# The query projection of six pairs of batches as seven block products, on one Trainium2 core

## The chip, the core and the metric

The kernel runs on one core of one Trainium2 chip. The core has five engines with a queue each: TensorE (PE; its weight loads are listed apart as PEld), VectorE (DVE), ScalarE (ACT), GpSimd (POOL) and SyncE (SP, which here only issues transfers). The metric is the device time of one execution in microseconds (us). Of before there are three timed runs and one profiled execution.

## The reference

All tensors are fp32. For each of 16 batches, with 100 rows `hidden` of 640 and 722 rows of 384, the last 4 of which are the tokens `ca` and the other 718 `enc`:

```python
query = hidden_states @ Wq                 # 100 x 640, 8 heads of 80
keyt, valt = enc @ Wk, enc @ Wv            # 718 x 640
hs = _mha(query, keyt, valt)
ca_q1 = jnp.einsum('btc,th->bch', ca, Wq_ca)[:, indices, :]     # 100 x 640
ca_hs1 = _mha(ca_q1, hidden_states, hidden_states)
ca_hs2 = _mha(ca_hs1 @ Wq, ca @ Wk_ca, ca @ Wv_ca)
out = (hs + ca_hs2) @ Wout + b_out + hidden_states
```

`_mha` is softmax attention by heads. The change concerns the first line, `hidden_states @ Wq`.

## The kernel before

The kernel is one loop over the 16 batches (`for b in range(B)`, line 1236), written for one order: from there on each engine runs its instructions in the order in which the program names them (`manual_schedule`, line 1235). TensorE, VectorE, ScalarE, Pool and SP meet only in semaphores that the framework sets where a buffer is written, read or given free.

One turn of the loop does, for batch b, the scores (`scores`, three groups of keys), the maximum over them (`Maximum`, `top`), their subtraction and exponential (`subtract`, `exponential`), the values (`Values`, `vv.go`), and for batch b + 1 the keys (`Keys`, `kk.go`, and `last_keys`). Keys and values are already computed by sums of blocks: `enc_sums` (line 481) makes thirteen sums of blocks of the encoder rows on Pool, into slots 7 to 14 of the tile `enc`, slots 0 to 6 of which come from memory by transfers (`load_enc`). That tile has two buffers: the one of batch b + 2 becomes free when the value products of batch b have read it. The output of pairs of row blocks is also made by sums (`Last.sums`, `project_pair`), in the turns after batches 2, 5, 7, 10 and 12 (`PAIRS`).

The second attention, over the 4 tokens, is the class `Second`. Its scores are made on Pool (`scores1`, lines 798 and 805), its first maximum on VectorE (`softmax1`, lines 700 to 730: a transpose, a reduction, two short groups of reductions, a spread copy, a transpose back; and the subtraction of line 815), its values on Pool (`values2`, lines 892 and 899: a product for each token and a sum). `load` issues the transfers of the first two tokens' values from Pool's queue; those of the other two are issued from SP's queue as tokens are used up.

**The queries.** Two batches share them. In each odd batch b the queries of the pair p + 1 (batches b + 1 and b + 2) are made (lines 1435 to 1438), after `last_keys` and, where there is one, `project_pair`, and before the attention product `a_ps` of line 1456. Just ahead of them in the program stand the key masks `keys(m_next)` and `enc_sums(enc_next)`, both on Pool alone. `queries` is called for five groups of 128 output columns. Each is five matmuls, one for each 128 of the 640 contracted rows, with a weight tile of 128 x 128 and both batches' rows, 2 x 100, as moving columns:

```python
for c in range(HC):
    nc.tensor.matmul(q_ps[...], wq_sb[:, c, n * P : (n + 1) * P], xT[:, :, c, :], ...)
```

Columns 0 to 511 hold the first 64 columns of each head, and go by a copy on ScalarE into `qp`; the last 128 hold the other 16 of each head, and go into `qz` by two products with a mask. `xT` holds both batches' rows, transposed, and `wq_sb` the weights.

PSUM is eight banks: two pairs (`pair`), two of `psumk`, two of `psum1`. The queries before take theirs from the last two in turn.

Other matmuls already use halves of the columns: `QC` cuts the attention's 100 rows into 0 to 63 and 64 to 99, and the preparation of the tokens' keys (line 1128) uses 64-column weight tiles at 0 and 64.

Of the kernel before, what the change touches and what calls it, by code (L numbers as in the profile page):

```python
# [18 lines left out]
P = 128  # L19
# [107 lines left out]
def kernel(  # L127
# [60 lines left out]
    def hs2_tile(name):  # L188
        return main.tile([P, H], F32, tag="hs2", name=name)
# [361 lines left out]
                )  # L551


    def chunk_keys(n, banks, weights, enc):
# [197 lines left out]
    class Second:  # L752
# [56 lines left out]
        def softmax1(self, n=8):  # L809

            if not self.top:
                self.top = Maximum(e1, f"1_{self.b}", self.b - 2 in PAIRS)
            self.top.go(n)
            if self.top.over is not None:
                nc.vector.tensor_tensor(e1[:S], e1[:S], self.top.over[:S], ALU.subtract)
# [64 lines left out]
            )  # L880
            self.p2 = p2

        def values2(self, behind=None):

            b, p2 = self.b, self.p2
            self.hs2 = hs2_tile(f"hs2_{b}")[:S]
            sums = self.hs2.rearrange("p (h d) -> p h d", h=NH)
            for t in range(T):
# [347 lines left out]
    for b in range(B):  # L1236
# [5 lines left out]
        def loads():  # L1242

            if b == 0:
                nc.sync.dma_start(
                    out=wout_sb, in_=wout.rearrange("(c p) n -> p c n", p=P)
                )
            if b + 2 >= B:
                return None, None
            x_next = xT_at[0] if b % 2 else load_x(p + 1)  # L1250
            xT_at[0] = x_next
            return Second(b + 2, x_next), load_enc(b + 2)
# [74 lines left out]
        elif b + 1 < B:  # L1327
# [59 lines left out]
            second_next, enc_next = loads()  # L1387
            if b + 2 < B:
                m_next = load_m(b + 2)
            subtract(2)  # L1390
# [6 lines left out]
            if last.b in PAIRS:  # L1397
                second.softmax1(3)
                last.project_pair()
                if last.b == max(PAIRS):  # L1400
# [40 lines left out]

# [37 lines left out]
        if b + 2 < B:  # L1479
            second_next.products()  # L1480
            second_next.copy()
        if 0 < b < B - 2:
            mine.turn()
        last = mine
# [55 lines left out]
```

## Time and profile before

| | before |
|---|---|
| timed runs, us | 924.89, 922.83, 924.90; median 924.89 |
| profiled execution, us | 925.05 |
| its span, us | 923.3 |
| granted TensorE clock | 1.00 |
| busy: TensorE, VectorE, Pool, ScalarE | 99%, 74%, 74%, 47% |

A row of the order of time reads: start in us, duration in us, engine, line, operation, output and inputs with their shapes, and how many were merged; in brackets the idle time before it and what ended it. A row of the chain that ended last reads: start, duration, engine, output, line, count. A row of stretches reads: the stretch, its length, then the busy time of TensorE, weight loads, VectorE, ScalarE and Pool with the instructions of each, the granted clock, the share of the transfer engines and what they moved. A matmul in fp32 leaves two records, one for each of two passes. For TensorE a shape such as 128*64 128x64 is rows and columns of the weights, and then rows and moving columns.

### The profile page before, as it was taken

To read this page: it belongs to the slowest core of one execution; us is meant where nothing else is said; L and a number is where in the kernel's file an instruction comes from. 1 tells how busy PE (TensorE), PEld (TensorE's weight loads), DVE (VectorE), ACT (ScalarE), POOL (GpSimd) and SP (SyncE) were. 2 spreads that over 40 slices of the span, in tenths; PEclk is the share of its full clock that TensorE was granted. 3 is DMA by queue.
4 is the path that set the end of the run, shared out by engine and by line. 5 is a ranking of instruction groups with operands and counts; after the bars stand their busy time and mean duration, and the time that the engine had idled before them with its cause. 6 is when DMAs were issued, how large, how long until landed. Compare 5 with 4: busy or idle time off the path is not lost.

```text
span 923.3 us, 26190 instructions
## 1 busy us (share of the span) xinstructions
PE 916.2 (99%) x11290; PEld 772.4 (84%) x11290; DVE 679.9 (74%) x1085; ACT 434.2 (47%) x836; POOL 682.1 (74%) x647
## 2 busy tenths in 40 slices
PE   9999999999999999999999999999999999999998
PEld 6988889788797979888798787988879888797866
DVE  2459795888739896795967859579883898838883
ACT  2234543737327373552636536264641737427341
POOL 5749999788947878497784968757996588956723
PEclk9999999999999999999999999999999999999999
DMA  8822013050300404032030310205031050310201
GB/s 258 262 94 78 25 43 100 2 156 2 103 31 13 116 3 131 3 92 65 19 115 4 103 54 30 76 2 154 3 90 43 2 155 2 104 45 2 82 20 41
DMA packets 49675, 62.85 MB, mean 68 GB/s; under 512 B 14072, under 2 KB 38200, under 8 KB 49560
## 3 DMA queue, kind: packets, MB, share of 16 engines
q1 hardware_dynamic: 45512, 51.49, 18.4%
q0 software_dynamic: 3024, 8.53, 3.0%
q8 instruction: 89, 1.46, 0.7%
q10 hardware_dynamic: 1024, 1.15, 0.4%
q14 instruction: 26, 0.21, 0.1%
HBM read 55.59 MB, written 5.57 MB: 66 GB/s over the span
## 4 chain that ended last, share of the span: by engine, by line
PE 96%; DVE 3%; DMA 1%; issue 0%; POOL 0%; ACTq 0%; DVEq 0%; POOLq 0%
PE a_ps L1456 12%; PE s_ps L609 12%; PE v_psA L434 10%; PE v_psB L434 8%; PE kT_ps L559 8%; PE k_psA L465 8%; PE q_ps L535 7%; PE k_psB L465 6%; PE o_ps L1050 5%; PE v_psC L434 3%; PE k_psC L465 3%; PE v_ps L375 2%; PE v_psD L434 2%; PE v_psE L434 2%; PE y_ps L773 1%; PE k_psD L465 1%
## 5 line engine op out<-in xcount | busy, mean ns | idle before, releaser
L798 POOL TENSOR_TENSOR e<-ca,g 100x800 f32<-100x800 f32 x64 | 97.9, 1540 | 125.1 <-ACT kT L407 82.1
L500 POOL TENSOR_TENSOR enc<-enc 128x240 f32<-128x240 f32 x135 | 109.5, 820 | 18.2 <-DMA enc<-in_enct 11.1
L1258 DVE TENSOR_TENSOR st<-st,over 120x1600 f32<-120x1600 f32 x48 | 119.1, 2482 | 0.0
L1456 PEld LDWEIGHTS a_ps<-vs,st 120*36 120x36 f32 (+3 forms) x3072 | 109.2, 125 | 4.9 <-issue 4.8
L1456 PE MATMUL a_ps<-vs,st 120*36 120x81 f32 (+3 forms) x3072 | 112.0, 233 | 0.0
L434 PE MATMUL v_psA<-wv_sb,enc 128*120 128x320 f32 x352 | 109.3, 433 | 0.0
L899 POOL TENSOR_TENSOR hs<-hs,hs 100x640 f32<-100x640 f32 x48 | 100.6, 2095 | 3.8
L805 POOL TENSOR_TENSOR e<-e,e 100x800 f32<-100x800 f32 x48 | 93.6, 1950 | 3.8
L892 POOL TENSOR_TENSOR hs<-vb,p 100x640 f32<-100x640 f32 x64 | 88.0, 1386 | 5.9 <-DMA vb<-va_d 3.0
L434 PE MATMUL v_psB<-wv_sb,enc 128*120 128x320 f32 x296 | 91.9, 433 | 0.0
L1266 ACT ACTIVATE st<-st 120x1600 f32<-120x1600 f32 x48 | 73.9, 1539 | 37.0 <-DVE st L1258 36.9
L465 PE MATMUL k_psA<-enc,wk_sb 128*128 128x240 f32 x360 | 89.2, 371 | 0.0
L434 PEld LDWEIGHTS v_psA<-wv_sb,enc 128*120 128x120 f32 x352 | 64.2, 183 | 25.0 <-issue 0.5
L465 PEld LDWEIGHTS k_psA<-enc,wk_sb 128*128 128x128 f32 x360 | 67.2, 190 | 15.0
L1270 DVE TENSOR_TENSOR most<-most,st 120x800 f32<-120x800 f32 x64 | 67.6, 1056 | 15.9 <-ACT st L659 14.8
L609 PE MATMUL s_ps<-qp,kT 64*56 64x100 f32 (+1 forms) x3072 | 73.5, 248 | 0.0
L465 PE MATMUL k_psB<-enc,wk_sb 128*128 128x240 f32 x300 | 73.0, 366 | 0.0
L434 PEld LDWEIGHTS v_psB<-wv_sb,enc 128*120 128x120 f32 x296 | 54.1, 183 | 21.9 <-DVE vs L405 0.4
L609 PEld LDWEIGHTS s_ps<-qp,kT 64*56 64x56 f32 (+1 forms) x3072 | 67.1, 130 | 5.5 <-issue 4.2
L965 ACT COPY hsT<-turned_hs 32x160 f32<-32x160 f32 (+7 forms) x244 | 67.7, 278 | 3.0
L535 PE MATMUL q_ps<-xT,wq_sb 128*128 128x200 f32 x400 | 69.1, 333 | 0.0
L535 PEld LDWEIGHTS q_ps<-xT,wq_sb 128*128 128x128 f32 x400 | 67.8, 190 | 1.0 <-issue 0.5
(168 smaller groups left out, 1766.1 us busy)
## 6 DMA issues: line engine op xcount, KB each, us to landing
vb<-va_d POOLq DMA_DIRECT2D x32, 250.0 KB, 3.8
vb<-va_d SPq DMA_DIRECT2D x32, 250.0 KB
enc<-in_enct SPq DMA_DIRECT2D x30, 240.0 KB
enc<-in_enct SPq DMA_DIRECT2D x15, 360.0 KB
xT<-in_xt SPq DMA_DIRECT2D x8, 500.0 KB
rest<-in_enct SPq DMA_DIRECT2D x31, 120.0 KB
xn<-in_x SPq DMA_DIRECT2D x11, 320.0 KB
out<-xn SPq DMA_DIRECT2D x11, 320.0 KB
```

Source lines behind the costliest of these rows:

```text
L434: nc.tensor.matmul(at[0][j][:KN, : H // 2], a_form(self.enc, f)[:, j * KN : (j + 1) * KN], wv_there.get(f, wv_sb[:, W_AT[f]]), start=first ...
L465: nc.tensor.matmul(at[:, i * KT : (i + 1) * KT], wk_sb[:, W_AT[f], i], a_form(self.enc, f), start=(first and i == 0), stop=last, skip_grou ...
L500: nc.gpsimd.tensor_tensor(out, left, right, op)
L535: nc.tensor.matmul(q_ps[:, : 2 * S].rearrange("p (j s) -> p j s", j=2), wq_sb[:, c, n * P : (n + 1) * P], xT[:, :, c, :], start=(c == 0), ...
L609: nc.tensor.matmul(s_ps[at][k0:k1, cols], w, rhs, start=not begun & {(at, k) for k in range(k0, k1, 32)}, stop=last, skip_group_check=True,)
L798: first = nc.gpsimd.tensor_tensor(to, self.ca[:, t, :].unsqueeze(1).to_broadcast([S, NH, S]), g[:, :, t].unsqueeze(2).to_broadcast([S, NH, ...
L805: nc.gpsimd.tensor_tensor(e, e, to, ALU.add)
L892: first = nc.gpsimd.tensor_tensor(to, self.vb[t][:S].rearrange("p (h d) -> p h d", h=NH), p2[:, :, t].unsqueeze(2).to_broadcast([S, NH, D] ...
L899: nc.gpsimd.tensor_tensor(sums, sums, to, ALU.add)
L1258: return nc.vector.tensor_tensor(st[i], st[i], top.over[:KN].unsqueeze(1).to_broadcast([KN, 2, ROWS]), ALU.subtract,)
L1266: nc.scalar.activation(st[i], st[i], AF.Exp, scale=SCALE)
L1456: nc.tensor.matmul(a_v[lo:hi, h % 4], st[i // 2][: KEYS[i], i % 2, h * S + lo : h * S + hi], block(i, h // 4)[: KEYS[i], h % 4], start=(i ...
```

## The change

In the odd batches 3 to 13 (the queries of the pairs 2 to 7) the product over the first 512 of the 640 contracted rows and the first 512 output columns is made of seven block products for eight, after Strassen and Winograd. The blocks are two halves of the contraction (256 rows, v(0, m) and v(1, m) of batch m), two halves of the output columns (W(c, g)), and the two batches. The sums are

- t1 = v(0,1) - v(0,0), t2 = v(1,1) - t1, t4 = v(1,0) - t2, t3 = v(1,1) - v(0,1), each 128 x 200;
- w2 = W'(1,0) - W(0,0), w3 = W(1,1) - w2, then w2 = W(0,1) - w2, each 128 x 512, where W'(1,0) = W(1,0) + W(1,1) is made once on VectorE at the end of batch 1 and stays in `wq_sb`.

All but that one are made on Pool, into the slots of the next `enc` tile that `enc_sums` fills later. The last 128 contracted rows (`rest`) and the last 128 output columns (bank f) are made as before. All matmuls of these queries have weight tiles of 64 columns, at 0 and 64 in turn. Six banks are used: two pairs (f and e, c and d) and both `psumk` (a and b). Banks a and b are read and then accumulated further, so each product that adds to them comes after a read. VectorE adds five times out of PSUM into `qp`.

The order changes with it. In these batches the transfers of `loads` are named ahead of `second.load`, and `enc_sums` comes after the queries. Where there is no `project_pair` (batches 5, 7, 9, `parted`) the sums stand between the third and the fourth token of `values2` on Pool; `second.load` and `keys(m_next)` come after the queries; and `softmax1` stops after three steps, its rest standing behind the read of bank b. In batches 3, 11 and 13 `keys(m_next)` stays ahead and the sums follow it, and `softmax1` is run to its end before.

```diff
+        def sums(self):
+            v = self.v
+            for out, left, right in (
+                (self.t1, v(0, 1), v(0, 0)),
+                (self.t2, v(1, 1), self.t1),
+                (self.w2, wq_block(1, 0), wq_block(0, 0)),
+                (self.t4, v(1, 0), self.t2),
+                (self.t3, v(1, 1), v(0, 1)),
+                (self.w3, wq_block(1, 1), self.w2),
+            ):
+                nc.gpsimd.tensor_tensor(out, left, right, ALU.subtract)
+
+        def product(self, bank, weights, moving, first):
+            steps = [(c, i) for c in range(weights.shape[1]) for i in range(2)]
+            for n, (c, i) in enumerate(steps):
+                for k in (0, 64):
+                    nc.tensor.matmul(
+                        bank[k : k + 64, i * S : (i + 1) * S],
+                        weights[:, c, i * P + k : i * P + k + 64],
+                        moving[:, c],
+                        start=first and n == 0,
+                        stop=n == len(steps) - 1,
+                        skip_group_check=True,
+                    )
+
+        def rest(self, bank, g, m, first):
+            weights = wq_sb[:, 4:, 2 * g * P : 2 * (g + 1) * P]
+            self.product(bank, weights, self.xT[:, m, 4:], first)
+
+        def make(self, tiles, between):
...
+            for ch in range(HC):
+                for k in (0, 64):
+                    nc.tensor.matmul(
+                        full(f)[k : k + 64],
+                        wq_sb[:, ch, 4 * P + k : 4 * P + k + 64],
+                        self.xT[:, :, ch, :],
...
+            for u in range(2):
+                nc.scalar.mul(
+                    qz[:, 0, :, u * S : (u + 1) * S], full(f), qmask[:, u : u + 1]
+                )
+            self.product(a, w(0, 0), v(0, 0), True)
+            nc.scalar.copy(q(0, 0), full(a))
+            self.rest(c, 0, 0, True)
+            self.product(c, w(0, 1), v(1, 0), False)
+            add(c, 0, 0)
+            self.product(a, self.w2, self.t2, False)
+            nc.gpsimd.tensor_tensor(self.w2, w(0, 1), self.w2, ALU.subtract)
+            self.rest(e, 1, 0, True)
+            self.product(e, w(1, 1), self.t4, False)
+            nc.scalar.copy(q(1, 0), full(e))
+            add(a, 1, 0)
+            self.product(b, self.w3, self.t3, True)
+            add(b, 1, 0)
+            self.rest(d, 0, 1, True)
+            self.product(d, self.w2, v(1, 1), False)
+            nc.scalar.copy(q(0, 1), full(d))
+            self.rest(b, 1, 1, False)
+            nc.scalar.copy(q(1, 1), full(b))
+            between()
+            self.product(a, w(1, 0), self.t1, False)
+            add(a, 0, 1)
+            add(a, 1, 1)
...
-            now.values2()
+            parted = b % 2 and b > 1 and last.b not in PAIRS
+            now.values2(None, range(T - 1 if parted else T))
...
-            second.load()
+            mixed = None
+            if b % 2 and b > 1:
+                second_next, enc_next = loads()
+                mixed = Queries(p + 1, xT_at[0], enc_next[0])
+            if parted:
+                mixed.sums()
+                now.values2(None, range(T - 1, T))
+            else:
+                second.load()
...
-            second.softmax1()
+            second.softmax1(3 if parted else 8)
...
-        if 0 < b < B - 2:
-            keys(m_next)
-            enc_sums(enc_next)
         if b % 2 and b + 1 < B:
             xT, tiles = xT_at[0], queries_tiles(p + 1)
-            for n in range(HC):
-                queries(p + 1, xT, tiles, n)
+            if not mixed:
+                for n in range(HC):
+                    queries(p + 1, xT, tiles, n)
+            elif parted:
+                mixed.make(tiles, second.softmax1)
+                second.load()
+            else:
+                keys(m_next)
+                mixed.sums()
+                mixed.make(tiles, second.softmax1)
+        if 0 < b < B - 2:
+            if not mixed or parted:
+                keys(m_next)
+            enc_sums(enc_next)
...
+        if b == 1:
+            nc.vector.tensor_tensor(
+                wq_block(1, 0), wq_block(1, 0), wq_block(1, 1), ALU.add
+            )
```

More of the change, by code (lines that the diff above doesn't have):

```diff
@@ L551, in queries, with wq_block, __init__, v @@
                 )
+    def wq_block(g, c):
+        return wq_sb[:, 2 * c : 2 * c + 2, 2 * g * P : 2 * (g + 1) * P]
+    class Queries:
+        def __init__(self, p, xT, enc):
+            self.p, self.xT = p, xT
+            room = enc[:, len(A_RAW) :].rearrange("p f k -> p (f k)")
+            part = lambda lo, n: room[:, lo : lo + 2 * n].rearrange(
+                "p (c n) -> p c n", c=2
+            )
+            self.w2, self.t1 = part(0, 2 * P), part(4 * P, S)
+            lo = 3 * KT
+            self.w3 = part(lo, 2 * P)
+            self.t3, self.t2, self.t4 = (
+                part(lo + 4 * P + 2 * i * S, S) for i in range(3)
+            )
+        def v(self, c, m):
+            return self.xT[:, m, 2 * c : 2 * c + 2]
+        def sums(self):
[25 more added lines that the diff above has]
+        def make(self, tiles, between):
+            qp, qz = tiles
+            p, v, w = self.p, self.v, wq_block
+            one = pair(f"q_ps1_{p}")
+            two = pair(f"q_ps2_{p}")
+            a, b = psumk(f"q_psA_{p}"), psumk(f"q_psB_{p}")
+            f, e, c, d = one[:, 0], one[:, 1], two[:, 0], two[:, 1]
+            def q(g, m):
+                return qp[:, g, :, m * S : (m + 1) * S]
+            def full(bank):
+                return bank[:, : 2 * S].rearrange("p (i s) -> p i s", i=2)
+            def add(bank, g, m):
+                nc.vector.tensor_tensor(q(g, m), full(bank), q(g, m), ALU.add)
+            for ch in range(HC):
[4 more added lines that the diff above has]
+                        self.xT[:, :, ch, :],
+                        start=(ch == 0),
+                        stop=(ch == HC - 1),
+                        skip_group_check=True,
+                    )
+            for u in range(2):
+                nc.scalar.mul(
+                    qz[:, 0, :, u * S : (u + 1) * S], full(f), qmask[:, u : u + 1]
+                )
+            self.product(a, w(0, 0), v(0, 0), True)
[20 more added lines that the diff above has]
+            add(a, 1, 1)
@@ L812, in softmax1 @@
                 self.top = Maximum(e1, f"1_{self.b}", self.b - 2 in PAIRS)
+            if self.top.over is not None:
+                return
             self.top.go(n)
```

11 lines of the change are left out of this document (7 added, 4 removed).

## The prediction

> **What bounds the kernel now.** I read the page first (span, busy shares, shares of the chain that ended last), then what TensorE waited for, then the chain in order of time around the block of queries, and last the order of time on each engine there.
>
> ```profile
> span 923.3 us, 26190 instructions
> PE 916.2 (99%) x11290; PEld 772.4 (84%) x11290; DVE 679.9 (74%) x1085; ACT 434.2 (47%) x836; POOL 682.1 (74%) x647
> PE 96%; DVE 3%; DMA 1%; issue 0%; POOL 0%; ACTq 0%; DVEq 0%; POOLq 0%
> PE idle_ps L1116 <- DVE idle L1113: 1.1, 1, 1.1
> PE y_ps L773 <- POOL m L745: 0.7, 1, 0.7
> ...
> PE k_psC L465 <- DVE vs L405: 0.4, 2, 0.2
> 253.94 8.46 PE q_ps L535 x50
> 262.40 6.92 PE a_ps L1456 x191
> ...
> 357.60 8.46 PE q_ps L535 x50
> 366.06 6.92 PE a_ps L1456 x191
> ```
>
> TensorE is busy in 916.2 of 923.3 us and is 96% of the chain; its longest waits are three one-off pieces of about 1 us or less, none at the queries. So a microsecond taken from TensorE's own stream is a microsecond of the span, and so is each new wait put into it. The block of queries is 8.46 us, 50 records (25 matmuls, two records each in fp32): 169.2 ns a record. With 200 moving columns that is 2 x 200 cycles of the 2.4 per ns that the granted clock of 1.00 stands for (166.7 ns) and 2.5 ns. The attention product follows at once, at 262.40 and 366.06. The last two rows are batch 5, the others batch 3.
>
> **What the change does to TensorE.** Six of the eight blocks (the odd batches 3 to 13) are redone. Five of the 25 matmuls (the last 128 output columns) keep 200 moving columns, in two 64-column halves. The other 20 become seven block products of four and four remainders of two matmuls of 100 columns, 36 in all, again in halves: 72 matmuls, 144 records. Full-width work falls from 25 x 200 = 5000 to 1000 + 3600 = 4600 columns, 8%. What is left of that hangs on the cost of a 64-column record with 100 moving columns, a shape that does not run now. Three neighbours do:
>
> ```profile
> L1128 PE MATMUL k_ps<-tokens,wk_sb x60: 222/222/270, 20.3 to 22.0; 128*64 128x64 f32 x60
> 366.06:372.98 6.92, 6.92 (x198) 6.92 (x200) 1.67 (x3) 1.50 (x3) 4.74 (x7) 1.00 0.02 5
> 273.08 2.97 PE L609 MATMUL s_ps<-qp,kT 64*64 64x100 f32 x128
> 275.98 0.95 PE L609 MATMUL s_ps<-qz,kT 32*120 32x200 f32 x16
> ```
>
> The first has the same weights (128 rows, 64 columns, both halves in turn) over 64 moving columns: 1.7 us between the first and last of 60 starts, 29 ns each. The second row is the attention product's window: by the code 8 heads x 6 blocks x 2 halves x 2 = 192 records of 81 columns in 6.92 us, 36.0 ns each. Both are N/2.4 + 2.3 ns, so two halves together advance as fast as one full-width record and only the 2.3 ns is paid twice. At N = 100 that is 44.0 ns. The scores give the dear end: 100 columns in four tiles, 128 records from 273.08 to 275.98, 22.7 ns each; a pair of halves as slow as those four is 45.3 ns a record. I take 44.0, the rows of the same tiling. The 200-column halves are 83.3 + 2.3 = 85.6 ns.
>
> One block: 144 x 44.0 = 6.34, and 20 x 85.6 = 1.71, together 8.05 us for 8.46: 0.41 us saved (0.22 at 45.3 ns). Six blocks: 2.46 us, dear end 1.3. Every block still starts after full-width work and ends before the attention's halves.
>
> The row against this is the weight load. *The Trainium skill ("TensorE: Matmul & The Clock Gate", section "LDWEIGHTS (loading the stationary operand)") has a load take its columns over 1.2 per ns, 53.3 ns for 64; were loads one after another, a record could not be faster than that.* In the first row above a load and a matmul of just this shape go by every 29 ns, and 29 is under 44, so loads do not decide here; it stays as a small rival.
>
> **The new waits.** Within a block, counted from its first record and with no wait: the 200-column part ends at 1.71, product one at 2.42, remainder and product on bank c at 2.77 and 3.47, the product with w2 at 4.18, remainder and product on e at 4.53 and 5.23, the one with w3 at 5.94, remainder d 6.29, the product with the second w2 6.99, remainder b 7.34, the last product 8.05. Sums are due at 3.47 (t2, w2), 4.53 (t4), 5.23 (t3, w3) and 6.29 (second w2, which can start only once the product with the first is over, at 4.18). They all come from Pool, in order with its other work:
>
> ```profile
> 249.74 1.54 POOL L1071 TENSOR_TENSOR wout<-wout,wout_sb 128x640 f32<-128x640 f32 x1
> 251.24 1.41 POOL L745 TENSOR_TENSOR m<-mb,hmask 128x64 f32<-128x64 f32 x5
> 252.61 0.69 POOL L500 TENSOR_TENSOR enc<-enc 128x240 f32<-128x240 f32 x1
> 255.82 1.08 DVE L815 TENSOR_TENSOR e<-e,over 100x800 f32<-100x800 f32 x1
> 341.99 1.78 DVE L1258 TENSOR_TENSOR st<-st,over 120x1600 f32<-120x1600 f32 x1
> 350.97 1.55 POOL L899 TENSOR_TENSOR hs<-hs,hs 100x640 f32<-100x640 f32 x1
> 351.91 1.24 PE L434 MATMUL v_psA<-wv_sb,enc 128*120 128x320 f32 x4
> 352.59 1.27 POOL L892 TENSOR_TENSOR hs<-vb,p 100x640 f32<-100x640 f32 x1
> 352.68 2.86 DVE L1258 TENSOR_TENSOR st<-st,over 120x1600 f32<-120x1600 f32 x1
> 353.94 3.02 POOL L899 TENSOR_TENSOR hs<-hs,hs 100x640 f32<-100x640 f32 x1
> ```
>
> From 0.69 us at 240 elements and 1.54 at 640 (2.1 ns an element) a 200-element sum is 0.60 and a 512-element one 1.27; with 0.05 between instructions the six take 4 x 0.65 + 2 x 1.32 = 5.24 us, the seventh 1.32. Pool and VectorE sums of two operands exclude each other: the subtraction of 1.78 us takes 2.86 where Pool's 1.27 us product began first, and Pool's next sum then takes 3.02 for 1.55.
>
> Batches 3, 11, 13 (keys first, then the sums): Pool is free at 251.24 + 1.41 = 252.65. The six end at 257.89, or 258.97 if the 1.08 us subtraction of 255.82 gets between. Due (253.94 + 5.23) 259.17. The seventh is ready at 260.29, due 260.23: 0.06 us late.
>
> Batches 5, 7, 9 (sums ahead of the last token's value): the scratch lies in the buffer that the value products read until 351.91 + 1.24 = 353.15, and the subtraction that starts at 352.68 holds Pool until 352.68 + 1.78 = 354.46. The six end at 359.70, the moved token (1.27 + 1.54 and gaps) at 362.66, the seventh at 363.98; due 357.60 + 6.29 = 363.89: 0.09 late.
>
> So the last Pool sum is the thin place: margin nothing, in both kinds. With a signal's way I book 0.08 us a block, 0.5 in all; the ends are none, and 0.5 us a block (3.0) if Pool is held once more for half of such a 1.08 us extension.
>
> **What is added off the path.** The rows that cover it:
>
> ```profile
> 245.42 0.49 DVE L1061 TENSOR_TENSOR xn<-o_ps,xn 128x320 f32<-128x320 f32 x1 [0.56 <-issue]
> 255.67 0.33 ACT L543 COPY qp<-q_ps 128x200 f32<-128x200 f32 x1 [8.95 <-PE q_ps L535]
> 358.26 1.30 DVE L712 TENSOR_REDUCE mx<-side 32x25 f32<-32x100 f32 x4
> 361.67 0.99 DVE L815 TENSOR_TENSOR e<-e,over 100x800 f32<-100x800 f32 x1
> 366.10 0.74 ACT L547 ACTIVATE qz<-q_ps,qmask 128x200 f32<-128x200 f32 x2 [1.36 <-PE q_ps L535]
> 366.73 0.87 ACT L818 ACTIVATE e<-e 100x800 f32<-100x800 f32 x1
> 369.65 0.18 DVE L1468 RECIPROCAL rs<-a_ps 100x4 f32<-100x4 f32 x1 [6.99 <-PE a_ps L1456]
> 372.80 0.93 PE L773 MATMUL y_ps<-m,xT 128*36 128x72 f32 x20
> 373.65 1.60 PE L609 MATMUL s_ps<-qp,kT 64*64 64x100 f32 x64
> 381.20 1.08 PE L465 MATMUL k_psA<-enc,wk_sb 128*128 128x240 f32 x4
> 384.56 3.03 POOL L798 TENSOR_TENSOR e<-ca,g 100x800 f32<-100x800 f32 x2 [13.44 <-ACT kT L407]
> 356.90 1.09 POOL L847 DMA_DIRECT2D vb<-va_d  x2
> 404.56 2.49 POOL L892 TENSOR_TENSOR hs<-vb,p 100x640 f32<-100x640 f32 x2
> ```
>
> ScalarE has the same four copies (0.33) and two masks (0.74 the pair), earlier: masks until about 2.55, the copy of bank a until 2.9, due 3.47. VectorE gets five additions out of PSUM, under 0.49 us each, about 0.4. The one that TensorE meets is the read of bank b: e's copy ends at 5.7, the addition to the same queries at 6.1, b's at 6.5, due 6.99. The maximum's three steps ahead of them end at 359.56, 2.0 into batch 5's block, and its rest (three steps of 1 us) is queued behind b's read: uncovered, it would have made that read 3 us late. It ends near 9.6, the exponential then at 10.5, where it is at 366.73 + 0.87 = 10.0 now; the two last additions end at 10.4, ahead of the scores at 373.65 (16.0) and of the reads of the attention's banks at 369.65 (12.0). The sum over the query weights in batch 1 (once, 512 elements, under 1 us) falls in VectorE's wait for the next scores, of which TensorE sees nothing.
>
> Pool does 5.24 + 1.32 us more in each of six batches. Behind the seventh sum, which waits for TensorE, stand in batch 5 the two transfers (1.09), the key masks (1.40) and thirteen sums (9.4): the masks end near 9.0, due at 372.80 (15.2), the sums near 18.5 to 20, while the first of them is due at 381.20 (23.6) and Pool's own next work at 384.56 (27.0). The moved transfers are used 47 us later, at 404.56. SP's queue keeps its order. All of this costs nothing unless Pool is over 4 us later than that.
>
> **The sum.** 2.46 saved - 0.5 waited = 2.0 us. The profiled execution took 925.05 us (its span 923.3 and 1.75 around it), 0.16 above the median of 924.89; so 923.05 in its terms and 922.9 against the median, 0.22% faster.
>
> **The rivals.**
>
> 1. *The gain is given back.* The dear record (1.3 us saved) with 0.2 to 0.5 us of waiting a block (1.2 to 3.0 us): 924.8 to 926.6, centre 925.2. For: the margins of 0. Against: TensorE now reads banks emptied by others all the time, with 0.4 us of wait in 923.
> 2. *Slower: the second w2 comes late.* It stands behind one more Pool job in batches 5, 7, 9 and behind the masks in 3, 11, 13, and TensorE cannot go round it. If Pool loses a whole 1.08 us to VectorE twice a block, the product is some 2 us after its time: +12 - 2.5, 934; once, 6.5 - 2.5, 928.9. It decides from 0.41 us of lateness a block. Against: after VectorE's big subtraction its work there is transposes, reductions and PSUM reads, and the Pool sums of 0.69 us beside such work are not stretched.
> 3. *Loads in single file.* 144 x 53.3 + 1.71 = 9.39 us a block, +0.93 x 6 = 930.5. Against it, the 29 ns.
> 4. *The halves do not run side by side* at 100 columns, so the change doesn't do what it says: a record at 85.6 costs 12.3 + 3.4 = 15.7 us a block, +43: 968. Against it, the 36.0 ns.
>
> **Chances.** Forecast 0.68, rival 1 0.16, rival 2 0.12, rivals 3 and 4 0.02 each. About 0.3% (2.8 us) is what a measurement of this kernel can tell from no change; the three runs of before lie 2.1 us apart. The forecast is 0.8 us short of that bound, so half of its share falls past it and half inside: faster 0.34; same 0.34 + 0.16 = 0.50; slower 0.16. Range 920.8 (the forecast less that spread of 2.1) to 926.6 (rival 1's end); the rest is left out.
>
> **What will show it.** Record starts of the new products 44 ns apart and a block of 8.1 us between its first record and the attention's: the tiling step holds. A TensorE wait for Pool at the product with the second w2 under 0.2 us: the margins hold; 0.5 or more: rival 2, and the Pool rows ahead of it will say which job was held. A wait for VectorE in the block would refute the read-ahead step, and one for Pool at the next batch's keys the claim that its late work is covered. A block over 8.46 us makes the prediction wrong.

## The result, and the profile after

| | before | changed |
|---|---|---|
| median, us (22 runs each) | 924.12 | 922.12 |
| lowest and highest, us | 922.39, 926.71 | 920.32, 925.14 |
| profiled execution and its span, us | 925.05, 923.3 | 922.65, 920.9 |

The ratio is 0.9981, with a 95% interval of 0.9972 to 0.9990: 0.19% faster, where 0.22% was forecast. The page of the changed kernel, where the prediction showed those of before (span, busy shares, the queue that brings TensorE's instructions with its packets, MB and share, and the shares of the chain):

```profile
span 920.9 us, 27684 instructions
...
PE 911.9 (99%) x11974; PEld 766.2 (83%) x11974; DVE 692.5 (75%) x1116; ACT 434.4 (47%) x836; POOL 723.6 (79%) x689
...
q8 instruction: 94, 1.54, 0.7%
...
PE 97%; DVE 1%; DMA 0%; POOL 0%; issue 0%; ACT 0%; SPq 0%; ACTq 0%; POOLq 0%
```

TensorE still bounds: 911.9 us busy where it was 916.2. The order of time on TensorE at the blocks of batch 3 and batch 5:

```profile
252.99 1.24 PE L1160 MATMUL o_ps<-wout,hsT 128*128 128x320 f32 x4
254.16 1.91 PE L625 MATMUL q_ps<-xT,wq_sb 128*64 128x200 f32 x20
255.90 0.86 PE L593 MATMUL q_psA<-xT,wq_sb 128*64 128x100 f32 x16
...
260.37 0.86 PE L593 MATMUL q_ps<-xT,enc 128*64 128x100 f32 x16
...
262.08 6.93 PE L1585 MATMUL a_ps<-vs,st 120*64 120x81 f32 x192
...
356.74 1.91 PE L625 MATMUL q_ps<-xT,wq_sb 128*64 128x200 f32 x20
...
362.95 0.86 PE L593 MATMUL q_ps<-xT,enc 128*64 128x100 f32 x16
...
364.66 5.52 PE L1585 MATMUL a_ps<-vs,st 120*64 120x81 f32 x152
```

From the first record of the block to the first of the attention it takes 262.08 - 254.16 = 7.92 us, and 364.66 - 356.74 = 7.92. The same view of the kernel before, batch 3:

```profile
252.70 1.24 PE L1050 MATMUL o_ps<-wout,hsT 128*128 128x320 f32 x4
253.78 8.62 PE L535 MATMUL q_ps<-xT,wq_sb 128*128 128x200 f32 x50
262.33 0.90 PE L1456 MATMUL a_ps<-vs,st 120*64 120x81 f32 x19
```

From start to start that is 8.55 us, so a block is 0.63 shorter. The chain of waits, from which the prediction took 8.46, goes from end to end, and in the changed kernel reads:

```profile
254.23 1.84 PE q_ps L625 x20
...
262.25 1.75 PE a_ps L1585 x49
```

That is 8.02 us. Ends of matmuls are modelled, so what follows goes by starts. No row inside the blocks has a bracket, so TensorE waits for nobody there. The 144 records with 100 columns take 262.08 - 255.90 = 6.18 us, 42.9 ns each, and the 20 with 200 columns 1.74 us. The 42.9 ns is a mean: in the trace the records of two halves start some 6 ns apart, and the next two 86 ns after them. Pool, and then VectorE, at the same places:

```profile
256.22 2.02 POOL L587 TENSOR_TENSOR enc<-wq_sb,enc 128x512 f32<-128x512 f32 x1
258.63 1.28 POOL L643 TENSOR_TENSOR enc<-wq_sb,enc 128x512 f32<-128x512 f32 x1 [0.40 <-PE q_psA L593]
...
357.20 1.27 POOL L587 TENSOR_TENSOR enc<-wq_sb,enc 128x512 f32<-128x512 f32 x1
...
361.28 1.27 POOL L643 TENSOR_TENSOR enc<-wq_sb,enc 128x512 f32<-128x512 f32 x1
...
383.17 3.04 POOL L905 TENSOR_TENSOR e<-ca,g 100x800 f32<-100x800 f32 x2 [7.83 <-ACT kT L407]
```

```profile
256.11 0.99 DVE L924 TENSOR_TENSOR e<-e,over 100x800 f32<-100x800 f32 x1
...
360.49 0.37 DVE L621 TENSOR_TENSOR qp<-q_ps,qp 128x200 f32<-128x200 f32 x1 [2.73 <-PE q_ps L593]
...
365.30 1.21 DVE L924 TENSOR_TENSOR e<-e,over 100x800 f32<-100x800 f32 x1
```

The second w2 is ready at 258.63 + 1.28 = 259.91 and used at 260.37; in batch 5 at 361.28 + 1.27 = 362.55 and 362.95. It has 0.46 and 0.40 us to spare. Pool still stands idle for 7.83 us ahead of its next own work.

Six blocks have become shorter by 0.63 us each, 3.8 in all, yet the time fell by 2.0 us. Most of what was given back shows in TensorE's waits (us in total, times, the longest):

```profile
PE z_ps L934 <- issue: 1.1, 3, 0.6
...
PE s_ps L716 <- issue: 0.6, 2, 0.5
...
PE a_ps L1585 <- ACT st L1376: 0.3, 1, 0.3
```

and at one place in the order of time:

```profile
643.35 0.62 PE L880 MATMUL y_ps<-m,xT 128*36 128x72 f32 x12
644.73 0.52 PE L880 MATMUL y_ps<-m,xT 128*64 128x108 f32 x8 [0.77 <-POOL enc L500]
```

These gaps stand in stages that the change doesn't touch. The Pool sum that the last bracket names makes `enc`, which y_ps does not read (it reads `m` and `xT`).

To part the two, take the stretch from the first query record of batch 1 (ahead of the first changed block) to the first score record of the last stage of scores. Its ends on TensorE, before and then changed:

```profile
140.49 2.73 PE L535 MATMUL q_ps<-xT,wq_sb 128*128 128x200 f32 x15
...
873.09 1.60 PE L609 MATMUL s_ps<-qp,kT 64*64 64x100 f32 x64
```

```profile
139.58 3.74 PE L535 MATMUL q_ps<-xT,wq_sb 128*128 128x200 f32 x21
...
869.98 1.60 PE L716 MATMUL s_ps<-qp,kT 64*64 64x100 f32 x64
```

The table has this stretch for the main kernels, measured in the same way; "gaps" is the sum of the idle times of 0.15 us or more in brackets of TensorE's rows there.

| kernel | stretch, us | gaps, us | without gaps |
|---|---|---|---|
| before | 732.60 | 0.60 | 732.0 |
| before, again | 732.41 | 0.75 | 731.7 |
| changed | 730.40 | 2.21 | 728.2 |
| changed, again | 729.50 | 1.10 | 728.4 |
| weight tiles of 64 alone | 734.95 | 2.29 | 732.7 |
| sums alone, unused | 734.00 | 1.91 | 732.1 |
| changed, instructions moved by 96 | 729.12 | 0.94 | 728.2 |
| changed, moved by 248 | 731.35 | 2.13 | 729.2 |
| changed, moved by 96, smaller start | 729.73 | 1.53 | 728.2 |
| before, moved by 176 | 732.61 | 1.13 | 731.5 |

Without gaps the changed kernel is 3.3 to 3.8 us shorter. By the blocks: 7.92 us for 8.55; the four o_ps records ahead of the block take 254.16 - 252.99 = 1.17 us instead of 253.78 - 252.70 = 1.08, as the change of tile shape now falls there and not behind the block; and the attention behind, up to the next scores, takes 0.05 less. That is -0.63 + 0.09 - 0.05 = -0.59, six times 3.5 us. The gaps take 0.35 (1.10 - 0.75) to 1.6 us (2.21 - 0.60) of it back. That is by brackets, which count too little, since the ends are modelled: in two of the runs below, waits of 0.84 and 0.96 us by their brackets made a block 1.06 and 1.18 us longer from start to start.

### The profile page after: what moved, and what is told of

Its sections match the earlier page's. It is cut to its first block, busy times and chain, and to the rows that moved or that the text cites. A ratio compares the mean times of both kernels' runs of the same rounds, so it can differ in the third digit from the quotient of the medians.

```text
span 920.9 us, 27684 instructions
## 1 busy us (share of the span) xinstructions
PE 911.9 (99%) x11974; PEld 766.2 (83%) x11974; DVE 692.5 (75%) x1116; ACT 434.4 (47%) x836; POOL 723.6 (79%) x689
## 3 DMA queue, kind: packets, MB, share of 16 engines
q8 instruction: 94, 1.54, 0.7%
## 4 chain that ended last, share of the span: by engine, by line
PE 97%; DVE 1%; DMA 0%; POOL 0%; issue 0%; ACT 0%; SPq 0%; ACTq 0%; POOLq 0%
PE s_ps L716 12%; PE a_ps L1585 11%; PE v_psA L434 11%; PE v_psB L434 9%; PE k_psA L465 8%; PE kT_ps L666 8%; PE k_psB L465 7%; PE o_ps L1160 5%; PE v_psC L434 4%; PE k_psC L465 3%; PE v_ps L375 2%; PE q_ps L593 2%; PE q_ps L535 2%; PE v_psD L434 2%; PE v_psE L434 2%; PE q_psA L593 1%
## 5 line engine op out<-in xcount | busy, mean ns | idle before, releaser
L500 POOL TENSOR_TENSOR enc<-enc 128x240 f32<-128x240 f32 x135 | 106.6, 800 | 18.2 <-DMA enc<-in_enct 11.1
L1368 DVE TENSOR_TENSOR st<-st,over 120x1600 f32<-120x1600 f32 x48 | 113.8, 2373 | 0.0
L1009 POOL TENSOR_TENSOR hs<-hs,hs 100x640 f32<-100x640 f32 x48 | 96.3, 2007 | 3.8
L1002 POOL TENSOR_TENSOR hs<-vb,p 100x640 f32<-100x640 f32 x64 | 90.3, 1421 | 3.7 <-DMA vb<-va_d 0.9
L772 ACT COPY st<-s_ps 120x800 f32<-120x800 f32 x64 | 49.8, 829 | 34.3 <-PE s_ps L716 34.3
L465 PEld LDWEIGHTS k_psB<-enc,wk_sb 128*128 128x128 f32 x300 | 57.0, 190 | 7.7
```

What stands on the lines that cost most here:

```text
L465: nc.tensor.matmul(at[:, i * KT : (i + 1) * KT], wk_sb[:, W_AT[f], i], a_form(self.enc, f), start=(first and i == 0), stop=last, skip_grou ...
L500: nc.gpsimd.tensor_tensor(out, left, right, op)
L1002: first = nc.gpsimd.tensor_tensor(to, self.vb[t][:S].rearrange("p (h d) -> p h d", h=NH), p2[:, :, t].unsqueeze(2).to_broadcast([S, NH, D] ...
L1009: nc.gpsimd.tensor_tensor(sums, sums, to, ALU.add)
L1368: return nc.vector.tensor_tensor(st[i], st[i], top.over[:KN].unsqueeze(1).to_broadcast([KN, 2, ROWS]), ALU.subtract,)
```

## The experiments

Each ratio is to the kernel before, timed beside that run (medians of 923.94 to 924.65 us). "Stream theory" in the expectations is the account so far: shorter blocks in TensorE's own stream shorten the time. "y_ps of batch 10" is the stage at 643 us above (turn 10 of the loop over the batches), and z_ps of batches 14 and 15 are the stages that start at 830 and 877 us.

**Both kernels again.** No edit.

> The changed kernel once more, for a second trace. Stream theory: the six blocks of queries are shorter by 0.59 us each, from the last full-width group ahead of them to the next batch's scores (17.29 to 16.70 us in batch 3), 3.5 us in all, and what is missing to that in the time (about 2 us) is gaps that fall elsewhere in each execution: the blocks again 0.59 us shorter, the gaps at other places, a ratio of 0.997 to 0.999. Rival, given back: the gaps come at the same batches again (ahead of the scores of batch 3, at the token products of batch 10), because Pool's added work is late there.

> The kernel before once more, for a second trace of it. Stream theory: a ratio of 1.000 within 0.001, blocks of 8.46 us as before, and gaps of TensorE of 1 to 3 us in all in the loop, at other places than in the first trace, where the trace showed 0.6 us. Rival, given back: again under 1 us of such gaps, so that those of the changed kernel (2.7 us) belong to the change.

The changed kernel: median 922.83 us of 11 runs against 923.94, ratio 0.9986 (0.9973 to 0.9999). Four of its gaps were in stages that had one in the first profile too, with other sizes: y_ps at 643 us 0.28 (0.77), s_ps at 756 us 0.42 (0.17), z_ps at 829 and 877 us 0.40 and 0.49 (0.22 and 0.28). The kernel before: ratio 0.9994 (0.9982 to 1.0005), and 0.75 us of gaps in the stretch, less than the 1 to 3 us expected of gaps that fall anywhere. So most places go with the program, and not, as the first expectation had it, with the execution; the sizes vary.

**Tiles of 64 columns alone**: the kernel before, its full products in halves for the six pairs.

```diff
+        wide_q = p < 2
...
-            nc.tensor.matmul(
-                q_ps[:, : 2 * S].rearrange("p (j s) -> p j s", j=2),
-                wq_sb[:, c, n * P : (n + 1) * P],
+            for k in (0,) if wide_q else (0, 64):
+                m = P if wide_q else 64
+                nc.tensor.matmul(
+                    q_ps[k : k + m, : 2 * S].rearrange("p (j s) -> p j s", j=2),
+                    wq_sb[:, c, n * P + k : n * P + k + m],
```

> The kernel before with the queries of the same six pairs in weight tiles of 64 columns, no block products and no sums: 100 records of 200 columns. Stream theory: 87 ns a record (the 20 records of that shape in the changed kernel take 1.74 us), 8.7 us a block for 8.46, less the 0.1 us that the step from full width to halves costs at either place: 0.1 to 0.25 us more a block, 0.6 to 1.5 us in all, a ratio of 1.0005 to 1.002. Rival, the tiling brings the gain: blocks shorter by 0.3 us or more, a ratio under 0.9985.

**Seven products with full tiles**: the changed kernel with weight tiles of 128 columns, in both loops.

```diff
-                for k in (0, 64):
+                for k in (0,):
                     nc.tensor.matmul(
-                        bank[k : k + 64, i * S : (i + 1) * S],
-                        weights[:, c, i * P + k : i * P + k + 64],
+                        bank[:, i * S : (i + 1) * S],
+                        weights[:, c, i * P : (i + 1) * P],
```

> The changed kernel with weight tiles of 128 columns: 72 records of 100 moving columns and 10 of 200 in place of 144 and 20. If a record costs only its moving columns (83.3 + 2.5 ns): 72 x 85.8 + 10 x 169.2 = 7.87 us a block, as short as with halves (7.92). If the weight load decides (the Trainium skill, TensorE: Matmul & The Clock Gate, section LDWEIGHTS, 128 columns over 1.2 per ns, 107 ns a load): 72 x 107 + 1.69 = 9.4 us a block, 1.5 us longer than with halves, 9 us in all, 3 to 7 us slower than before.

TensorE around the block of batch 3 in order of time, first with halves alone, then with full tiles:

```profile
253.88 1.24 PE L1054 MATMUL o_ps<-wout,hsT 128*128 128x320 f32 x4
255.05 8.68 PE L538 MATMUL q_ps<-xT,wq_sb 128*64 128x200 f32 x100
263.56 6.93 PE L1460 MATMUL a_ps<-vs,st 120*64 120x81 f32 x192
```

```profile
254.33 1.24 PE L1160 MATMUL o_ps<-wout,hsT 128*128 128x320 f32 x4
255.40 1.85 PE L625 MATMUL q_ps<-xT,wq_sb 128*128 128x200 f32 x10
257.09 1.03 PE L593 MATMUL q_psA<-xT,wq_sb 128*128 128x100 f32 x8
...
265.20 0.98 PE L1585 MATMUL a_ps<-vs,st 120*64 120x81 f32 x22
```

Halves alone: a block of 8.51 us, and 255.05 - 253.88 = 1.17 for the o_ps records ahead of it, where the full tiles have 255.40 - 254.33 = 1.07. From the o_ps records to the next scores it takes 17.29 us, as before the change. So the tile shape alone gains nothing. The kernel takes 926.09 us (12 runs), ratio 1.0024 (1.0009 to 1.0038), with 2.29 us of gaps, the largest at the same y_ps as in the changed kernel (its waits on TensorE):

```profile
PE y_ps L777 <- issue: 1.2, 1, 1.2
```

Full tiles: 265.20 - 255.40 = 9.80 us a block, longer than the eight products of before. 72 records take 265.20 - 257.09 = 8.11 us, 112.6 ns each, where a pair of halves takes 2 x 42.9 = 86 ns. The time is 932.13 (5 runs), ratio 1.0094 (1.0078 to 1.0109). At 100 moving columns a 128-column tile isn't bound by its moving columns any more: by the full-width record of 169.2 ns for 200 it would take 83.3 + 2.5 = 85.8 ns. By the rule of the Trainium skill ("TensorE: Matmul & The Clock Gate", section "LDWEIGHTS (loading the stationary operand)") 128 columns load in an estimated 106.7 ns, near the 112.6, so the weight load is the likely bound, though no run here changed the load alone; the 53.3 ns that the rule gives for 64 columns does not hold here as a bound, since a record goes by every 42.9 ns. So seven products pay only with halves: the two parts of the change need each other.

**The sums alone**: the kernel before, its queries as they were, with all seven Pool sums made in the changed kernel's order and never read (`again` is the second w2).

```diff
+            if parted:
+                mixed.sums()
...
+            elif parted:
+                for n in range(HC):
+                    queries(p + 1, xT, tiles, n)
+                mixed.again()
+                second.softmax1()
+                second.load()
```

> The changed order with its seven Pool sums at each of the six blocks, but the queries by the 25 full-width matmuls of before, which do not read the sums (the sum over the query weights at the end of batch 1 is left out, so the outputs stay the reference's). It prices Pool's 6.5 us a block alone. Stream theory: covered, a ratio of 1.000 within 0.001, and no wait of TensorE for Pool at the token products or the keys. Rival, given back: 1 to 2 us slower than before, 1.001 to 1.002.

The ratio is 1.0004 (0.9993 to 1.0015), blocks 8.55 us. Pool's work of some 6.5 us a block, and its later masks and sums, cost TensorE nothing that this run can tell, and its trace has no wait for Pool in the stretch.

**Pool later by one sum**: w3 is made twice.

```diff
                 (self.w3, wq_block(1, 1), self.w2),
+                (self.w3, wq_block(1, 1), self.w2),
```

> The changed kernel with the sum w3 made twice, so that Pool is 1.3 us later from there on. In the trace of the changed kernel the second w2 is ready 0.4 us ahead of its product in both kinds of batch. Theory of the thin margin: TensorE waits 1.3 - 0.4 = 0.9 us for Pool at that product (in batches 3, 11 and 13 some 0.5 us of it already at the product with w3), 5 us in all over the changed kernel, so 2 to 4 us slower than before, ratio 1.002 to 1.005. Rival, Pool has more room than that row says: under 0.3 us a block, ratio under 1.000.

Batch 5 in order of time, on Pool and on TensorE:

```profile
363.70 1.27 POOL L644 TENSOR_TENSOR enc<-wq_sb,enc 128x512 f32<-128x512 f32 x1
```

```profile
365.03 0.91 PE L594 MATMUL q_ps<-xT,enc 128*64 128x100 f32 x16 [0.84 <-POOL enc L644]
```

929.17 us (6 runs), ratio 1.0051 (1.0034 to 1.0069). The second w2 is ready at 364.97, and the product with it starts at 365.03, after 0.84 us of idle time. Of the 1.27 us that the sum took, 0.4 went into the margin and 0.84 into the wait: the margin of 0.40 above is real, and it is all there is. From start to start the block takes 8.98 us for 7.92. In batches 3, 11 and 13 the blocks took 8.61 to 8.66 us.

**The maximum ahead of the block**: `softmax1` is run to its end in batches 5, 7 and 9 before the queries.

```diff
-            second.softmax1(3 if parted else 8)
+            second.softmax1()
```

> The changed kernel with the whole maximum of batches 5, 7 and 9 ahead of the block on VectorE, and no rest behind the read of bank b. By the prediction the reads would come up to 3 us late (it called them uncovered): TensorE waits for VectorE in three blocks, up to 2.5 us each, some 7 us slower than the changed kernel. Rival, by the changed kernel's trace: VectorE stands idle for 2.7 us ahead of its first addition there, which takes in the rest of 3.0 us but for 0.3 us, and that addition has no reader for 2 us: the same time as the changed kernel, ratio 0.997 to 0.999, no wait for VectorE.

VectorE, Pool and TensorE in order of time, batch 5:

```profile
359.65 3.54 DVE L924 TENSOR_TENSOR e<-e,over 100x800 f32<-100x800 f32 x1
363.12 0.35 DVE L621 TENSOR_TENSOR qp<-q_ps,qp 128x200 f32<-128x200 f32 x1
```

```profile
359.57 1.54 POOL L1009 TENSOR_TENSOR hs<-hs,hs 100x640 f32<-100x640 f32 x1
```

```profile
363.52 0.56 PE L593 MATMUL q_ps<-xT,wq_sb 128*64 128x100 f32 x8 [0.96 <-DVE qp L621]
```

927.36 us (10 runs), ratio 1.0032 (1.0018 to 1.0045). The wait is 0.96 us, once a block, and each of the three blocks takes 9.10 us for 7.92. TensorE meets it not at bank b but at the remainder d, which waits for the addition out of bank c beside it. The maximum's last subtraction took 3.54 us, where the changed kernel has 1.21: it started 0.08 us after a Pool sum of 1.54 us and ended after the next one, the second w2 (361.07 + 1.28).

**A seventh pair**: the block products in batch 1 too.

```diff
-            if b % 2 and b > 1:
+            if b % 2:
...
-        if b == 1:
+        if b == 0:
```

> The changed kernel with the block products in batch 1 too (the pair of batches 2 and 3), the sum over the query weights moved to the end of batch 0. Stream theory: one more block shorter by 0.59 us, if Pool, which has other work in batch 1, has its sums ready: ratio 0.0006 under that of the changed kernel, which timing can hardly tell; the block's length in the trace tells. Rival: in batch 1 a sum is late and the block waits for Pool, 0.5 us or more.

```profile
151.08 1.60 PE L593 MATMUL q_psA<-enc 128*64 128x100 f32 x16 [6.08 <-POOL enc L587]
```

930.61 us (6 runs), ratio 1.0061 (1.0044 to 1.0078). In that batch Pool comes to the sums only after its values, three transfers and the masks, and TensorE waits 6.08 us for t2 and w2; the block takes 16.00 us for 8.58. Where the sums are not ahead, one block costs more than six gain.

**Instructions moved.** A matmul in fp32 is four instructions on TensorE, two weight loads and two multiplications, and the queue q8 brings 256 of them in each packet of 16 KB. The trace of the changed kernel has 24148 records of TensorE and its queue, 94.3 times 256, and q8 brought 94 packets. So each gap has a place within its packet, counted from TensorE's first record (the place of the packet's own end in this count isn't in the traces). In the 14 traces of this document TensorE has 53 gaps of 0.15 us or more after 100 us in the stages z_ps (32), s_ps (9), y_ps (8) and a_ps (4), and every one stands at place 192 or 193 of 256; of its 15 other gaps there, waits for VectorE or Pool, none does. The gap in y_ps at 643 us stands at 193. The view of transfers of the changed kernel for 640 to 648 us (a digit for each 0.2 us, the busy share of the 16 DMA engines in tenths):

```profile
DMA  9899999999660000000000000000200000000000
...
q1 hardware_dynamic: 393, 0.74, 26.2%
q8 instruction: 2, 0.03, 1.5%
```

The loads on q1 fill most of the DMA engines until 642.4 us, the first of the two packets starts at 642.31, as they end, and TensorE goes on 2.42 us later, at 644.73; during the gap itself nothing is on its way.

The theory ahead of the next runs was that TensorE stalls where a packet ends in a stage of short matmuls, and it can be moved: idle matmuls added at the start shift all that follows.

```diff
     for _ in range(5):
         nc.tensor.matmul(idle_ps[:, :P], idle, idle, start=True, stop=True)
+    for n in range(44):
+        k = 64 * (n % 2)
+        nc.tensor.matmul(
+            idle_ps[k : k + 64, :16],
+            idle[:, k : k + 64],
+            idle[:, :16],
```

That is the kernel before with 44 more; the changed kernel was run with 24 and with 62.

> The kernel before, with 44 small idle matmuls more at its start (176 of TensorE's instructions, 256 of which make one packet of 16 KB). They cost about 88 records x 29 ns = 2.6 us at the start, of which some 0.4 falls into the wait there for a load: 926 in all. Packet theory (TensorE stalls where the end of a packet falls into a stage of short matmuls): counted by instruction, y_ps of batch 10 now stands to the end of a packet as in the changed kernel, so a gap of 0.3 to 1.2 us appears there (that is where the changed kernel shows 0.28 to 0.77 and the kernel before none), perhaps one at y_ps of batch 8 too; gaps at z_ps of batches 2 to 15 vanish, since no packet ends late in any of them. Rival (the gap at y_ps of batch 10 belongs to the new order on Pool and VectorE): no gap there, gaps as before. Blocks of queries 8.55 us by both.

> The changed kernel with 24 small idle matmuls more at its start (96 instructions of TensorE, 1.4 us, about 1.0 of it not covered there). Packet theory: no packet ends in y_ps of batch 10 and none late in z_ps of batches 2, 5, 12, 14 and 15, where the changed kernel had its gaps; candidates that are left are z_ps of batch 9 and y_ps of batches 4 and 7. Gaps after the first query fall from 1.6 to 2.8 us to under 0.8, so the span behind the start is 1 to 2 us shorter, and the time 922 to 923 with the longer start. Rival: the gap at y_ps of batch 10 stays, and the time is 1 us longer, 923.5.

> The changed kernel with 62 small idle matmuls more at its start (248 instructions of TensorE, nearly a whole packet; 3.6 us, about 3.2 of it not covered there). Packet theory: ends of packets fall where they did in the changed kernel, 8 instructions earlier in each stage: gaps at y_ps of batch 10 or 13 and at z_ps of some of batches 2, 5, 12, 14 and 15, 1.5 to 3 us in all, as in the changed kernel without the addition. Rival (more idle work at the start changes the gaps, wherever packets end): gaps as in the kernel with 24 more, under 0.8. The time is 925.5 by the first.

The kernel before, moved by 176 instructions, in order of time on TensorE (all its gaps after batch 1):

```profile
650.99 0.96 PE L773 MATMUL y_ps<-m,xT 128*64 128x72 f32 x20 [0.34 <-issue]
...
765.06 0.87 PE L773 MATMUL y_ps<-m,xT 128*36 128x72 f32 x17 [0.79 <-issue]
```

The gap has come to the stage that had none in this kernel, without any of the change's work on Pool or VectorE, and a second one to the next but one y_ps; both stand at place 193. The one at z_ps, which the first profile of before had and the second had not, is not there. The rival falls. In y_ps of batch 8, at 547 us, where the expectation saw a second gap as possible, no place 193 falls and no gap shows; and the y_ps stages at 377 and 490 us show none although place 193 falls in them.

The changed kernel moved by 96 has no gap left in y_ps or z_ps. Its waits:

```profile
PE k_psA L465 <- DVE kT L405: 1.5, 1, 1.5
...
PE a_ps L1595 <- issue: 0.7, 1, 0.7
...
PE k_psC L465 <- DVE vs L405: 0.3, 1, 0.3
```

The stretch is 729.12 us, the shortest of all, 3.3 to 3.5 less than before: nearly the whole gain of the blocks. Moved by 248, nearly a packet, the gaps are back: 0.90 us at the same y_ps, four more, 2.13 us in all. So gaps follow the packets and not the idle work. The times were not what was expected: 925.54 us (12 runs, ratio 1.0009, 0.9999 to 1.0019) and 932.46 (6 runs, 1.0070, 1.0050 to 1.0090), and 930.75 (6 runs, 1.0056, 1.0043 to 1.0070) for the kernel before. An idle record took 53 to 57 ns at the start, not 29, and the first keys waited for VectorE (the first row above), which neither kernel shows without the addition: outside the stretch these three take 194.4 to 199.2 us, where the kernel before takes 189.0 and 190.7.

**Why only some packets cost time.** The start of every packet of q8 is in the traces. In all 53 gaps TensorE goes on 2.26 to 2.83 us after the transfer of a packet began, and there are two kinds. In the 32 gaps of z_ps no other transfer is on its way, and TensorE has run through the 256 instructions from the same place of the packet before in 2.57 to 3.33 us. In the 21 gaps of s_ps, y_ps and a_ps this took 4.36 to 4.64 us, but the packet began only 2.25 to 3.45 us after that place, while other transfers filled 87% or more of the DMA engines. So by the traces a gap comes where the next packet is late: because a stage uses up its instructions so fast, or because loads hold the packet up. After 100 us place 192 falls into these four stages 842 times in the 14 traces, and most often the packet is there in time. This is read from the traces; no run moved the loads.

**A smaller start.** The five large idle matmuls are replaced by 29 small ones, again 96 instructions more.

```diff
-    for _ in range(5):
-        nc.tensor.matmul(idle_ps[:, :P], idle, idle, start=True, stop=True)
+    for n in range(29):
```

> The changed kernel with 29 small idle matmuls at its start in place of the 5 large ones: 96 of TensorE's instructions more, as with 24 added, but 58 x 57 = 3.3 us where the large ones took 2.5, so about 0.8 us later at the start, of which 0.4 falls into the wait for a load. Packet theory: packets end where they did with 24 added, so the gaps from the first query of batch 1 on are again under 1 us and stand at none of y_ps of batch 10 and z_ps of batches 14 and 15; the way from there to the end is 3.5 us shorter than in the kernel before, and the time 921 to 922. Rival (that run's few gaps were chance): gaps of 1.6 to 2.8 us, and 922.5 to 923.5.

```profile
PE a_ps L1593 <- issue: 1.3, 2, 0.9
...
PE k_psA L465 <- DVE kT L405: 1.1, 1, 1.1
```

923.86 us (12 runs), ratio 0.9994 (0.9985 to 1.0003), no better than the changed kernel itself. y_ps and z_ps have no gap, as counted, but a_ps has two, 1.3 us in all, and the wait at the first keys stays. Neither forecast of the gaps' size was met: they come to 1.53 us, and the stretch is 2.7 to 2.9 us shorter than before, not 3.5. No kernel of these beats the changed one.

## Why the prediction was right

The time was right, a ratio of 0.9981 where 922.9 of 924.89 is 0.9978, but as the sum of a larger gain and of a loss that the forecast did not have; that the two came so near to 2.0 us is luck.

- *TensorE bounds* held: 99% busy, 97% of the chain. With blocks shorter by 0.59 us, 3.5 in all, the stretch without gaps is 3.3 to 3.8 us shorter.
- *The record of 44.0 ns* was mis-sized: 42.9, which is N/2.4 + 1.2. Over 144 records that is 0.16 us; the 20 wide ones took 1.74 us for 1.71. So a block is 7.92 us of records and not 8.05, 0.54 less than the 8.46 of before. The change of tile shape, which was to cost nothing net, moved: it took the 0.09 us between 8.46 and 8.55 behind the block, and takes 0.09 ahead of it now, with 0.05 less in the attention. In all a block saves 0.59 us, not 0.41; six blocks 3.5, not 2.46. The full-tile run shows what was left unsaid: that the halves are what makes seven products pay.
- *Pool's last sum, 0.06 to 0.09 us late* failed: it is 0.46 and 0.40 us early. In batch 5 the six sums end at 357.20 + 1.27 - 356.74 = 1.73 us into the block, where 2.10 was forecast, and the moved token and the seventh sum follow without the gaps of 0.05 to 0.1 us that were booked. In batch 3 the six end at 256.22 + 2.02 - 254.16 = 4.08 us, where 5.03 was booked with VectorE's subtraction between, and the seventh then waits 0.40 us for TensorE. The 0.5 us in all were not paid. That it is the thin place held: one sum later makes the block 1.06 us longer in batch 5.
- *Pool and VectorE exclude each other* held: the sum at 256.22 took 2.02 us for 1.27, beside VectorE's subtraction that began at 256.11. The 0.75 us are less than the 1.08 booked.
- *The read-ahead* held in kind: no wait with it, one without it. Its worth was a wait of 0.96 us and 1.18 us of block length, not 3. VectorE stands idle for 2.73 us ahead of its first addition, so most of the three steps found room even when run at once; what made them late was the subtraction stretched to 3.54 us. And it was the read of bank c that TensorE met, not that of bank b.
- *Pool's late work is covered* held: 7.83 us of idle time are left, and the sums alone cost nothing (ratio 1.0004).
- *The sum* lacked a term: the gaps where an instruction packet comes late. The change adds 342 matmuls, 1368 instructions, and moves all later stages against the packets; the gaps in the stretch rose from 0.60 and 0.75 us to 2.21 and 1.10. That is the first rival in kind, a gain partly given back, by a way that it did not name; its times, 924.8 us and more, were not reached. How much of the rise belongs to the change stays open: the sums alone have the TensorE instructions of before and 1.91 us of gaps, 1.58 of them in z_ps, so gaps come and go there in one and the same program. The one in y_ps at 643 us moves with the instructions, as the moved kernels show. The term also explains most of why the halves alone, with the same 17.29 us around each block, are 0.24% slower: gaps make 1.5 to 1.7 of the 2.35 to 2.55 us by which their stretch is longer. The rest was not traced.

2.46 - 0.5 = 2.0 was forecast; 3.5 less 0.35 to 1.6 is 1.9 to 3.2, and the medians say 2.0 and 1.1. The rest, the time outside the stretch, varies between profiles of one kernel: 190.7 (923.3 - 732.6) and 189.1 us (921.5 - 732.41) in the kernel before, 190.5 and 190.1 in the changed one.

## What to carry to other kernels

Here a product with fewer multiplications paid on TensorE only where each record was bound by its moving columns: before the count of columns is cut, look at what a record costs at the smaller size, and at whether halves of the weight columns load beside each other. Where TensorE is 99% busy, part of a small gain can vanish in stages that the change does not touch; measure a stretch with its gaps and without them before the change itself is blamed, and see at which instruction of its packet each gap stands. A wait that needs a whole sum's delay before it shows is found by delaying that sum.

## What the runs showed of the hardware

At one place in each 256 of TensorE's instructions (192 or 193, counted from its first record), in stages of short matmuls, TensorE stood still for 0.17 to 1.19 us, until 2.26 to 2.83 us after the transfer of a packet had begun; adding instructions ahead moved or removed these gaps. The Trainium skill ("Runtime: NRT & Kernel Launch", section "Instruction fetch mechanics") has the same 16 KB blocks of 256 instructions, and calls the cost of crossing one mostly hidden; here the packets agree (q8 brought 94 in 1.54 MB), and it is mostly hidden too, with three to five gaps in the stretch of the changed kernel, but the rest is as large as the gain that was looked for. When it isn't hidden is told above, from the traces; whether moving the loads away from these places would remove the gaps was not tried. The wait at the first keys, 1.1 to 1.6 us, came with every longer start and in two other kernels too; its cause was not tried.

A full-tile record with 100 moving columns took 112.6 ns, and two half-tile records, the same work, 86 ns. At the change from full tiles to halves the four full-tile records ahead of it took 0.09 to 0.10 us more (1.17 for 1.07 or 1.08).
